# Block 1's norm, transposition and first projection moved into the written-out head, with a new rank table

## The chip, the cores and the metric

One core of one Trainium2 chip runs the kernel. The metric is the device time of one execution in microseconds (us), the median of several runs. The core has a matrix engine (TensorE, in the profile PE for the matmuls and PEld for the loads of their weights), three engines for element-wise work (VectorE is DVE, ScalarE is ACT, GpSimd is POOL), and SyncE (SP), which here only issues data transfers (DMAs). Each engine works through its own list of instructions in order and waits for the others through semaphores. Matmul results go to PSUM, a small memory of eight banks; everything else lies in SBUF.

## What is computed

Input x has 4 sequences of 512 tokens with 256 features. A Mamba layer and a mixture of experts follow one another, each with a layer norm in front and behind and a residual sum:

```python
def _mamba_forward(h, in_proj_w, conv_w, conv_b, x_proj_w, dt_proj_w, dt_proj_b, A, D, out_proj_w):
    x, gate = split(einsum('bld,ed->ble', h, in_proj_w), 2)       # 256 -> 512 + 512
    xt = silu(causal_depthwise_conv4(x) + conv_b)
    ts, Bm, Cm = split(xt @ x_proj_w.T, [16, 32])                 # 16 + 16 + 16
    dt = softplus(ts @ dt_proj_w.T + dt_proj_b)
    state = state * exp(dt * A) + dt * Bm * xt                    # per token, 512 x 16 states
    y = (state @ Cm + xt * D) * silu(gate)
    return y @ out_proj_w.T
def _ffn(xt, ...):
    probs = softmax(xt @ w_router); top 4 of 16 experts, weights normalised -> cw
    g = silu(xt @ we1) * (xt @ we3) * cw;  moe = g @ we2          # hidden 128 per expert
    shared = silu(xt @ ws1) * (xt @ ws3) @ ws2                    # hidden 512
    return shared / 5 + moe * 4 / 5
x = x + layernorm(mamba(layernorm(x)))
x = x + layernorm(ffn(layernorm(x)))
```

All of it is in float32.

## The kernel before

**Blocks.** The 2048 tokens are worked on in 8 blocks of 256 tokens, two per sequence (blocks 0 and 1 are the halves of the first sequence, so block 1 takes over the last three columns of block 0's projection for its convolution, the `tail`, and block 0's last scan states, the `carry`).

For each block n there are these groups of steps:

- The **front**: `stats` (DVE, line 348), `rstd` (four small POOL operations, 354 to 357), `norm` (two ACT passes, 362), `transpose` (PE, 672), `evict` (the ACT copy of the transposed block out of PSUM into `xn_t`, 675), `pad0` (POOL writes the first three columns of the padded tile `xp`, 691 or 693), `in` (PE, 398; two halves m, each four matmuls, which PE carries out as eight instructions), `tail` (the ACT copy into `xp`, 696, and where the sequence goes on the copy of its last columns, 699), `conv` (PE, 413), `sigmoid` (ACT), `silu` (DVE, 430), `x_proj` (PE, 441), `ssm` (ACT, 449), `dt` (PE, 464), `softplus` (ACT, 470), `inputs` (POOL), the gate's `gin`, `gsig`, `gate` (PE 398, ACT 753, DVE 757), and transfers through DRAM that turn the data round (`xg`, `rep`, `bc`).
- The **scans**: 32 slots for each block. A slot takes two exponentials on ACT (`exps`, 500), half of a 128x1024 product on POOL (`dbx`, 512), one scan on DVE (`scan`, 795), one product on DVE (`hc`, 803), and a sum over states on PE (`sum`, 817).
- The **chain**: output projection (PE, 912), norm, residual sum, norm, transposition, the copy `evict2` (ACT, 945), router, and the experts' weights.
- The **experts**: ten steps of two experts each. A step is `h1` and `h3` (PE, 1059), `act` (ACT), `gated` (DVE, 1078), `weighted` and `product` (POOL, 1074 and 1081), and `down` (PE, 1094).

**Who sets the order.** Two parts of the program are ordered in different ways. The **head**, the function `first()`, is written out by hand: it loads the constants, and carries block 0 through its whole front and its first two `exps` and `dbx`. Everything later is a list of **tasks**. Each task has an engine, an estimated duration, the tasks it depends on, the buffers it takes and a **rank**. The planner (`Plan.order`) plays the list through with its own estimates and always takes the task that can start soonest on its engine; within a task's `patience` (in us) a task of lower rank may come first. The result is fixed before the program runs: each engine gets its instructions in the planned order and waits in that order.

A task's rank is the slot at which it is due, plus a shift that the tables `SHIFTS` hold for each kind of task and each block, plus what `NUDGES` holds for one task alone (the table is empty here):

```python
shift, patience = shift_of(name)
rank += shift + NUDGES.get(name, 0.0)
```

So that the planner knows what the head leaves behind, `did(...)` enters tasks as already done.

**Warm-ups.** `warm(n, bank)` (line 320) multiplies the unit matrix n times and throws the result away; each of these matmuls is two PE instructions. The head calls it in places where PE would have nothing to do, and until the first `down` the planner's last loop adds such matmuls wherever its plan leaves PE idle (those go to the bank `po`).

**Buffers.** Tiles with a name share a ring of a fixed number of buffers (`RINGS`): the bank `h` (three PSUM banks for the exponentials and scans), `o` (one), `g` (three, for the experts), `x` (three input blocks), `xn`, `xn_t`, `xp` and others.

**The head's order of loads.** x(0) first, half by SP and half by ACT; ACT then issues both halves of `w_in`; SP issues `chan`, `w_x`, `one_row`, `w_dt`, `a_rep`, `rsel`, `bsel`, then x(1) and x(2), then `w_out` and `w_r`.

Of the kernel before, what the change touches and what calls it, by code (L numbers as in the profile page):

```python
# [9 lines left out]
F32 = mybir.dt.float32  # L10
# [4 lines left out]
P = 128  # L15
# [4 lines left out]
KC = 4  # L20
# [37 lines left out]
    fA=(-0.25, -42.5, 4.25, -39, 39.75, -19.75, 44.5, -1.5),  # L58
    fB=(0, -35.25, -36, 6, 17.25, 55, -7.75, -55),
    fC=(-18.5, -59.25, 7.25, 1.5, -0.5, -12.75, -18, 3.25),  # L60
    fD=(28.25, 18.5, -1, -3.25, 0.25, 38.5, 0.75, -10),
    exps=(3, 34.75, 26.75, -5, -49.5, 44.75, -3.75, 0),
    dbx=(25.75, 11.75, -1.75, -1, 2, 17, 2.75, 12.5),
    scan=(46.75, 18, -13.25, 52, 58.5, 38.75, 48.5, 14.25),
    hc=(8, -37.75, 60, -8, 11, 49.25, -3.75, -17.25),
    keep=(54.75, 0, 25.75, 0, 31.5, 0, 35.75, 0),
    sum=(-18.25, -0.5, 0, 0, 5.25, -6.25, -13.25, 3),
    close=(1.75, 20.5, 2.5, -42.75, -34, 19.5, -5.5, 29),
    ld=(1.25, 34, 20, -0.25, -1.75, -17.5, 33, -9.75),
    bc=(1, 15, 1.5, -14.25, -33.5, 7.5, -5.75, 5),  # L70
    chain=(-4, -7.75, -47.75, -48.25, -17, -9, 8.25, 5.5),
    load=(-8, 9, -14.25, -51.25, -48.5, -60, -23.25, -20.25),
    h1=(60, 18.25, -37.75, -7.75, 9.75, 6.5, 5.75, 6),
    h3=(17.5, 38.75, -48, -19.5, -1.5, -0.75, -1.5, -22.5),
    act=(0, 49.5, 16.5, 3, 4.25, -3, 8.75, 8.25),
    gated=(-11.75, 3, -2, -9.25, 6.75, 2.5, 8.25, 15.5),
    prod=(57, -58.5, 38.75, -3.25, -9.5, -8.25, 0, -11.75),
    down=(-5, 48.5, -31.75, 14.75, -7.25, 6, -1.75, 47.5),
    fin=(16.25, 7, 24.5, 18.25, -2.25, 36.5, -3, 16),
# [3 lines left out]
    fA=(0.1, 0.3, 1.5, 0.1, 1.5, 0.1, 1, 0.1),  # L83
    fB=(0.1, 0.1, 0.1, 0.3, 0.1, 1.5, 1, 0.6),
    fC=(0.1, 0.1, 0.6, 1, 0.3, 0.1, 0.1, 0.1),
    fD=(2.2, 0.1, 0.1, 0.1, 0.1, 1, 0.1, 0.1),
    exps=(0.1, 2.2, 0.3, 0.1, 1.5, 0.3, 0.3, 0.3),
    dbx=(0.3, 0.1, 0.1, 0.1, 0.1, 0.1, 0.1, 2.2),
    scan=(1, 0.6, 0.1, 0.6, 2.2, 0.1, 0.1, 0.1),
    hc=(0.1, 0.1, 2.2, 2.2, 0.3, 0.6, 1.5, 0.1),  # L90
    keep=(1.5, 0.1, 0.1, 0.1, 0.6, 0.1, 1, 0.1),
    sum=(0.3, 1.5, 0.1, 0.1, 0.1, 0.1, 0.1, 0.1),
    close=(0.1, 0.3, 0.3, 0.6, 0.3, 0.3, 0.6, 0.6),
    ld=(1, 1, 1.5, 0.6, 1.5, 0.1, 2.2, 0.6),
    bc=(0.6, 2.2, 0.1, 1.5, 1.5, 0.3, 2.2, 0.6),
    chain=(0.6, 0.6, 0.3, 0.6, 0.1, 0.6, 0.1, 1.5),
    load=(2.2, 1.5, 1, 1.5, 2.2, 2.2, 0.1, 0.1),
    h1=(2.2, 0.3, 0.3, 0.1, 1, 0.1, 0.1, 2.2),
    h3=(0.1, 1, 0.1, 0.1, 0.3, 0.1, 1, 0.3),
    act=(0.1, 2.2, 0.1, 0.3, 0.6, 1, 0.1, 0.1),  # L100
    gated=(0.6, 0.1, 1, 0.6, 0.6, 0.1, 0.3, 0.1),
    prod=(1, 0.1, 1, 0.1, 0.1, 0.1, 0.1, 0.3),
    down=(0.3, 1.5, 0.1, 1, 0.1, 2.2, 0.1, 0.1),
    fin=(0.3, 1, 2.2, 1, 0.6, 2.2, 1.5, 0.1),
# [3 lines left out]

# [143 lines left out]
def mamba_then_moe(ctx: ExitStack, tc: tile.TileContext, a: dict, out: bass.AP):  # L252
# [28 lines left out]
    nc.sync.dma_start(out=chan, in_=a["chan"].rearrange("(c p) k -> p c k", p=P))  # L281
    w_x = const.tile([P, CI, P // 2], F32, name="w_x")
# [17 lines left out]
    for n in range(1, 3):  # L300
        load_x(n)
# [89 lines left out]
    def to_rep(n, m, w, t):  # L391
        nc.sync.dma_start(out=live[n]["rep"][ts(m, 2), :, w].rearrange("j p t -> p j t"), in_=t)

    def in_proj(n, m, bank):
        t = q["in", n, m] = ps.tile([P, 2, U], F32, name=bank)
        for j in range(2):
            for k in range(CD):
                T.matmul(  # L398
# [898 lines left out]
```

## Time and profile before

| what | value |
|---|---|
| median of 3 runs | 695.48 us (695.46 to 695.65) |
| the profiled execution | 695.37 us |
| its span, first to last instruction | 693.6 us |
| mean granted TensorE clock | 0.998 |
| busy: PE, PEld, DVE, ACT, POOL | 674.0, 536.5, 579.3, 495.5, 602.5 us |
| first scan of block 0, first scan of block 1 | 27.0, 96.5 us |
| first expert matmul | 119.6 us |
| last scan | 612.4 us |
| last matmul ends | 688.2 us |

In the views of the profile, a line of the timeline gives the start, the duration, the engine, the line of the kernel, the operation, what it writes and reads, shapes and a count; what stands in brackets is how long the engine was idle before it and who released it. A q behind an engine's name means its sequencer, which issues transfers. Instructions on one engine overlap a little, since they are pipelined; two matmul instructions of 256 columns start 0.216 us apart, though each is shown with 0.38 us.

### The profile page before, as it was taken

What the parts mean: (1) busy time and instruction counts of PE and PEld (TensorE: products, weight loads), DVE (VectorE), ACT (ScalarE), POOL (GpSimd) and SP (SyncE); (2) the same over time, 40 slices, a digit from 0 to 9 for tenths busy, and PEclk for the clock granted to TensorE, in tenths of its full rate; (3) what the DMA queues carried; (4) which work ended last, traced back from release to release, by engine and by line L of the source; (5) the groups of instructions that cost most, each with busy time, mean ns of one, the idle gap of its engine ahead of it and who ended that gap; (6) DMA issues with size and microseconds to landing.
All of it is one profiled execution on the core that took longest, in us unless ns stands there. A gap on an engine that the chain in (4) does not pass through costs nothing.

```text
span 693.6 us, 13321 instructions
## 1 busy us (share of the span) xinstructions
PE 674.0 (97%) x4462; PEld 536.5 (77%) x4462; DVE 579.3 (84%) x821; ACT 495.5 (71%) x1308; POOL 602.5 (87%) x607
## 2 busy tenths in 40 slices
PE   8999898999999999999999999999999999999996
PEld 7867676777878678877777788787777787878885
DVE  3799999999999899999999999889999979952112
ACT  2799979888768778877798867877777757724320
POOL 1597679999999999999999999999999999985553
PEclk9999999999999999999999999999999999999999
DMA  5398675686877596787678867686787764664561
GB/s 175 127 341 283 215 239 172 204 262 186 280 245 226 194 307 236 230 282 265 191 247 276 272 192 228 219 277 231 240 255 251 264 230 140 196 204 131 189 206 46
DMA packets 84840, 155.28 MB, mean 224 GB/s; under 512 B 9858, under 2 KB 33410, under 8 KB 84772
## 3 DMA queue, kind: packets, MB, share of 16 engines
q1 hardware_dynamic: 83940, 153.13, 67.9%
q10 hardware_dynamic: 832, 1.31, 0.5%
q8 instruction: 35, 0.57, 0.3%
q14 instruction: 33, 0.27, 0.1%
HBM read 135.40 MB, written 19.01 MB: 223 GB/s over the span
## 4 chain that ended last, share of the span: by engine, by line
PE 48%; DVE 10%; ACT 7%; POOL 3%; issue 2%; DMA 1%; POOLq 0%; DVEq 0%; ACTq 0%
PE h L1059 25%; PE po L1094 12%; DVE h L795 5%; PE y L817 4%; ACT h L500 3%; DVE hc L803 3%; PE f L912 2%; POOL dbx L512 1%; PE f L1094 1%; PE f L398 1%; DVE q L1078 1%; DMA rep<-rep 1%; PE f L413 1%; ACT h L503 1%; PE f L951 0%
## 5 line engine op out<-in xcount | busy, mean ns | idle before, releaser
L795 DVE TENSOR_TENSOR_SCAN h<-h,dbx 128x512 f32<-128x512 f32 x256 | 308.5, 1221 | 12.0 <-ACT h L503 6.4
L512 POOL TENSOR_TENSOR dbx<-rep,bt 128x1024 f32<-128x1024 f32 x127 | 299.6, 2362 | 13.3 <-DVE h L795 12.8
L1059 PE MATMUL h<-xn_t,w 128*128 128x256 f32 x1280 | 296.0, 382 | 0.2
L500 ACT ACTIVATE h<-rep,a_rep 128x256 f32<-128x256 f32 x512 | 244.5, 478 | 54.7 <-DVE hc L803 42.5
L1059 PEld LDWEIGHTS h<-xn_t,w 128*128 128x128 f32 x1280 | 239.4, 190 | 43.4 <-issue 4.4
L803 DVE TENSOR_TENSOR hc<-h,ct 128x512 f32<-128x512 f32 x256 | 171.6, 683 | 3.8 <-ACT carry L807 1.1
L1094 PE MATMUL po<-w,g 128*128 128x256 f32 x600 | 144.2, 383 | 1.0 <-POOL g L1081 0.8
L1094 PEld LDWEIGHTS po<-w,g 128*128 128x128 f32 x600 | 111.6, 190 | 22.5 <-POOL g L1081 3.9
L1081 POOL TENSOR_TENSOR g<-g,q 128x512 f32<-128x512 f32 x80 | 101.7, 1271 | 5.2 <-DVE q L1078 2.5
L1074 POOL TENSOR_TENSOR g<-g,cwb 128x512 f32<-128x512 f32 x64 | 81.4, 1271 | 19.4 <-ACT g L1071 15.6
L1078 DVE SCALAR_TENSOR_TENSOR q<-th,h 128x512 f32<-128x512 f32 x80 | 54.5, 681 | 49.2 <-PE h L1059 40.4
L1066 ACT ACTIVATE th<-h 128x512 f32<-128x512 f32 x80 | 47.5, 593 | 38.7 <-PE h L1059 38.3
L817 PE MATMUL y<-hc,sel 128*32 128x256 f32 x1024 | 67.5, 385 | 0.0
L817 PEld LDWEIGHTS y<-hc,sel 128*32 128x32 f32 x1024 | 27.5, 109 | 29.0 <-issue 14.6
L503 ACT COPY h<-zero 128x1 f32<-128x1 f32 x256 | 41.7, 163 | 8.2
L398 PE MATMUL f<-xn_t,w_in 128*128 128x256 f32 x176 | 42.6, 385 | 2.2 <-DVE gate L757 1.1
L1071 ACT COPY g<-h 128x512 f32<-128x512 f32 x64 | 37.1, 580 | 9.2 <-PE f L1094 8.7
L398 PEld LDWEIGHTS f<-xn_t,w_in 128*128 128x128 f32 x176 | 32.6, 190 | 10.1 <-ACT xn_t L675 1.7
L807 ACT COPY carry<-h 128x2 f32<-128x2 f32 x128 | 19.8, 160 | 19.2 <-DVE hc L803 13.5
L413 PE MATMUL h<-xp,taps 64*64 64x256 f32 x288 | 29.5, 381 | 0.8 <-DVE xt L430 0.8
L912 PE MATMUL f<-w_out,yg 128*128 128x256 f32 x112 | 26.5, 383 | 1.0 <-DVE xt L430 1.0
L413 PE MATMUL f<-xp,taps 64*64 64x256 f32 x208 | 25.4, 382 | 1.7 <-DVE xt L430 0.9
(178 smaller groups left out, 624.6 us busy)
## 6 DMA issues: line engine op xcount, KB each, us to landing
w<-in_w SPq DMA_DIRECT2D x80, 512.0 KB, 4.9
rep<-rep SPq DMA_DIRECT2D x124, 256.0 KB, 4.5
w<-in_w SPq DMA_DIRECT2D x80, 256.0 KB, 3.8
cwb<-cwd SPq DMA_DIRECT2D x64, 256.0 KB, 4.7
xg<-xg SPq DMA_DIRECT2D x32, 256.0 KB, 4.3
bt<-bc SPq DMA_DIRECT2D x8, 512.0 KB, 5.8
ct<-bc SPq DMA_DIRECT2D x8, 512.0 KB, 5.3
xg<-xt SPq DMA_DIRECT2D x16, 256.0 KB, 4.6
```

Source lines behind the costliest of these rows:

```text
L398: T.matmul(t[:, j, :], w_in[:, k, ts(2 * m + j, P)], q["xn_t", n][:, k, :], start=k == 0, stop=k == CD - 1,)
L413: T.matmul(t[j][half[r ^ j], :], taps[half[r], 2 * m + j, k, :], q["pad", n, m][half[r], j, k : k + U], start=k == 0, stop=k == KC - 1,)
L500: S.activation(h[:, j, :], dt[:, m, 0, :], AF.Exp, scale=a_rep[:, c, g, m : m + 1])
L512: G.tensor_tensor(t[:, m], reps[n * CI + c][:, m, 1, :], bt[:, m], ALU.mult)
L795: V.tensor_tensor_scan(flat, flat, dbx[:, ts(p, NJ), :].rearrange("p j t -> p (j t)"), 0.0, ALU.mult, ALU.add)
L803: V.tensor_tensor(hc, expo[k], ct, ALU.mult)
L817: T.matmul(ys[n, c][m * CS : (m + 1) * CS, :], sel, hcs[k][:, j, :], start=g == 0, stop=g == SG - 1,)
L1059: T.matmul(t[:, j, :], weights[i][:, j, ts(CD * w + k, P)], x[:, k, :], start=k == 0, stop=k == CD - 1,)
L1074: G.tensor_tensor(gs[i], gs[i], cws[i], ALU.mult)
L1078: V.scalar_tensor_tensor(t, hid[i, "th"], 1.0, hid[i, 1], ALU.add, ALU.mult)
L1081: G.tensor_tensor(gs[i], gs[i], hid[i, "q"], ALU.mult)
L1094: T.matmul(acc[n][t] if n == N - 1 else acc[n][:, t, :], gs[i][:, j, ts(t, P)], weights2[i][:, j, :], start=m == 0 and j == 0 and (t == 0 ...
```

## The change

The head takes over the first steps of block 1, and the planner's tables are replaced.

1. x(1) is loaded behind `chan`, ahead of `w_x`, instead of behind `bsel`.
2. In the head, block 1's statistics and `rstd` are put behind block 0's normalization; its two normalizing ACT passes (into a tile of the ring `o`) behind `make_taps()`; its transposition (into a bank `h`) behind block 0's convolutions; its copy into `xn_t` on DVE (into a tile of the ring `g`) behind `silu(0, 0)`. ACT did this copy before.
3. The first half of block 1's input projection, `in(1, 0)`, is cut into its four matmuls. One goes behind the second, one behind the fourth column of block 0's `x_proj`, each followed by two warm-ups, where four and two warm-ups were; the other two go behind `dt_proj`. The copy into `xp` is made by DVE, and the two warm-ups on `y` are gone. POOL copies both halves' tails into `xp`.
4. The planner no longer has `stats`, `rstd`, `norm`, `transpose`, `evict`, `pad0` of block 1 nor `in` and `tail` of its first half; `did` tells it so.
5. All values of `SHIFTS` and `PATIENCE` are new, and `NUDGES` gets some 90 entries.

```diff
 SHIFTS = dict(
-    dbx=(25.75, 11.75, -1.75, -1, 2, 17, 2.75, 12.5),
-    scan=(46.75, 18, -13.25, 52, 58.5, 38.75, 48.5, 14.25),
-    chain=(-4, -7.75, -47.75, -48.25, -17, -9, 8.25, 5.5),
-    h1=(60, 18.25, -37.75, -7.75, 9.75, 6.5, 5.75, 6),
+    dbx=(-4, -5, 51, 30.25, 46.5, 55, 30.75, 48.5),
+    scan=(45.25, 60, 0, 48.75, 46.75, 60, 23.5, 33.75),
+    chain=(-36, -22.75, -16, -28.25, 17.5, -47.75, -1, -4.5),
+    h1=(-4, 60, 53, 40.5, 57.25, -19, -6, 4.75),
...
 NUDGES = {
+    ("rep", 0, 1, 0): 6.5, ("xg", 0, 0, 1): 19.5, ("conv", 1, 1): -23.5, ("inputs", 1, 1): -24,
+    ("pad0", 2, 0): 2, ("gsig", 2, 1): -24.5, ("stats", 3): 13.25, ("in", 3, 1): 11.75,
...
 }
...
     nc.sync.dma_start(out=chan, in_=a["chan"].rearrange("(c p) k -> p c k", p=P))
+    load_x(1)
...
-    for n in range(1, 3):
-        load_x(n)
+    load_x(2)
...
-    def in_proj(n, m, bank):
-        t = q["in", n, m] = ps.tile([P, 2, U], F32, name=bank)
+    def in_parts(n, m, t):
+
+        q["in", n, m] = t
         for j in range(2):
             for k in range(CD):
                 T.matmul(
                     t[:, j, :], w_in[:, k, ts(2 * m + j, P)], q["xn_t", n][:, k, :],
                     start=k == 0, stop=k == CD - 1,
                 )
+                yield
+
+    def in_proj(n, m, bank):
+        for _ in in_parts(n, m, ps.tile([P, 2, U], F32, name=bank)):
+            pass
...
+        mr = rstd_of(stats_of(xs[1]))
         xn_t = q["xn_t", 0] = ring(work, [P, CD, U], "xn_t")
...
         make_taps()
+        xn1 = ring(work, [P, NU, D], "o")
+        normalize(xn1, tiles_of(xs[1]), mr)
...
             conv(0, m, (("po", "f"), ("h1", "h3"))[m])
+        t = ps_e.tile([P, CD, U], F32, name="h")
+        for k in range(CD):
+            for i in range(NU):
+                T.transpose(t[:, k, ts(i, P)], xn1[:, i, ts(k, P)], ident)
         sigmoid(0, 0)
         silu(0, 0)
+
+        q["xn_t", 1] = ring(work, [P, CD, U], "g")
+        V.tensor_copy(q["xn_t", 1], t)
...
         silu(0, 1)
+        parts = in_parts(1, 0, ps_e.tile([P, 2, U], F32, name="h"))
+        for m in range(2):
+            xp = q["pad", 1, m] = ring(work, [P, 2, KC - 1 + U], "xp")
+            G.tensor_copy(xp[:, :, 0 : KC - 1], tails.pop((1, m)))
+
+        def some(c):
+            next(parts)
+            warm(2, "f")
+
         S.activation(spare, zero, AF.Softplus)
-        x_proj(0, "y", lambda c: warm(5 - c, "f"))
+        x_proj(0, "y", some)
...
         dt_proj(0, ("po", "h1"))
+        for _ in parts:
+            pass
+        V.tensor_copy(q["pad", 1, 0][:, :, KC - 1 :], q["in", 1, 0])
         b0 = ps.tile([P, U], F32, name="f")
...
         V.tensor_copy(first_b, b0)
-        warm(2, "y")
         softplus(0)
...
-        if n:
+        if n > 1:
             if n > 2:
                 once(key("x"), "SP", 0.5, lambda: load_x(n), (), [("x", key("x"))], (), 256)
...
-            for m in range(2):
+            for m in range(n == 1, 2):
```

## The prediction

> **What bounds the kernel now.** I read the chain that ended last first, then busy time by stage, then the timeline of the head and of the first scans. The chain is mostly TensorE:
>
> ```profile
> PE 48%; DVE 10%; ACT 7%; POOL 3%; issue 2%; DMA 1%; POOLq 0%; DVEq 0%; ACTq 0%
> ```
>
> One table over four stretches: the head up to the first scan, block 0's scans up to the first expert matmul (119.60), up to the last scan, and the rest. Columns: length, then busy us (and instructions) of PE, PEld, DVE, ACT, POOL, then clock, DMA share, GB/s.
>
> ```profile
> 0.00:27.00 27.00, 24.86 (x199) 20.77 (x200) 11.39 (x36) 11.86 (x24) 4.20 (x15) 1.00 0.51 157
> 27.00:119.60 92.60, 83.57 (x754) 63.82 (x752) 88.22 (x118) 81.89 (x227) 75.34 (x83) 1.00 0.74 243
> 119.60:612.40 492.80, 489.59 (x3133) 386.68 (x3134) 461.09 (x632) 381.55 (x1020) 478.25 (x457) 1.00 0.72 235
> 612.40:694.00 81.60, 75.99 (x381) 65.25 (x379) 18.59 (x40) 20.25 (x39) 44.66 (x54) 0.98 0.49 158
> ```
>
> From 119.60 PE stands 492.80 - 489.59 = 3.2 us in 493, with POOL 14.6 behind it. So the end is: the time at which expert work starts, plus all PE work left then, plus few stalls, plus 5.4 (last matmul 688.2 to 693.6). Before 119.60 PE is not full: idle 92.60 - 83.57 = 9.0, and 146 of its instructions there are warm-ups (L320), 18 of which take 2.17 us, so 146 x 0.112 = 16.4. That is 25.4 us of spare PE, because DVE (88.22 of 92.60) paces block 0's scans.
>
> A second bound is close. Block 7's last scan starts at 612.4, its router input is copied at 632.2, and ten steps of h1, h3 and down at 3 x 1.73 us follow: 632.8 + 51.9 = 684.7, against PE's real end of 688.2. Whatever saves PE more than 3.5 us must also bring the last scan forward.
>
> **The head, part by part.** The added work: statistics of x(1) (DVE 0.70, row L348), four small POOL operations (0.19, 0.22, 0.71, 0.20; 1.5 with gaps, seen for block 2 at 32.16), two normalizing ACT passes (1.09), eight transposing PE instructions (0.47), a 512-wide DVE copy out of PSUM (0.69, row L540), eight input-projection PE instructions (8 x 0.216 = 1.73), the copy to xp (DVE 0.69), two tail copies (POOL 0.32). Removed there: 4 warm-ups, 8 PE instructions (0.9 us).
>
> The load of x(1) is now the third on SP's queue instead of after bsel. The nearest row is w_x, issued at 1.64 and landed 5.9 us later at 7.5, when the 1 MB of w_in on ACT's queue was through. x(1) is 256 KB, 128 KB more; at the some 350 GB/s of 3 to 7 us that is +0.4: 7.9. DVE asks for it at 8.03, between xn and xn_t. Late x(1) would hold the xn_t copy (8.69), behind which taps and the projection queue; bounds 7.1 (half of 350 GB/s from 5.66, where w_in's first half had landed) and 9.5 (after w_in, at the 127 GB/s of the page's second slice); I take no delay. w_x and the constants slide by 0.7 at most: w_x then lands at 8.3, used at 16.61; rsel (10.93), used at 22.02. [...]
>
> Statistics then end at 8.73, POOL at 10.3, the ACT passes at 11.4, which pushes the ACT copy to xp from 10.93 to 11.4; it ends at 12.0, before the convolution's 12.55. That much is covered. The transposition lies in PE's 0.38 wait before 16.61, and its rest ahead of the second x_proj column (17.0). Not covered is this:
>
> ```profile
> 16.48 0.47 DVE L430 SCALAR_TENSOR_TENSOR xt<-f,chan,sig 128x256 f32<-128x256 f32 x1
> 16.87 0.28 DVE L551 TENSOR_SCALAR sig<-sig 128x256 f32<-128x256 f32 x1
> 17.25 0.88 DVE L430 SCALAR_TENSOR_TENSOR xt<-h,chan,sig 128x256 f32<-128x256 f32 x2
> 17.37 1.16 PE L320 MATMUL f<-ident 128*128 128x128 f32 x8
> 18.46 0.66 PE L441 MATMUL y<-xt,w_x 128*64 128x128 f32 x8
> 19.05 0.71 PE L320 MATMUL f<-ident 128*128 128x128 f32 x4
> 19.17 0.37 ACT L449 ACTIVATE ssm<-y,one_row 128x128 f32<-128x128 f32 x1
> 26.39 0.70 DVE L348 BATCH_NORM_STATS2 st<-x 128x6 f32<-128x512 f32 x1
> 27.01 2.32 DVE L795 TENSOR_TENSOR_SCAN h<-h,dbx 128x512 f32<-128x512 f32 x2
> ```
>
> The new copy stands on DVE between silu(0,0) and sig: 16.95 to 17.65. sig goes to 17.65, silu(0,1) ends at 18.85 instead of 18.13. On PE the first projection matmul waits for that copy to 17.9 and lasts 0.43, two warm-ups 0.45, so x_proj's second half starts at 19.0, not 18.46 (+0.55), and ssm with it. The second matmul with its warm-ups (0.88) stands ahead of dt_proj: 19.0 + 0.6 + 0.88 + 0.1 = 20.6 against 19.69 (+0.9). Two more (0.86) and b0 (0.44) precede the spread matmuls, whose softplus comes 0.9 later too: 23.1 against 22.05, **+1.05** for everything up to the first scan. Bounds: 0 (if the order hides all) and 1.7 (all 1.73 exposed). Against it: x(1)'s statistics held DVE from 26.39 until the first scan, although that scan's dbx was there at 26.10 and the last rep copy ended at 26.47; they are gone: **-0.5**. Head: +0.5.
>
> **The stream.** Block 1 no longer takes there ACT 1.09 + 0.59 + 0.56 = 2.2, POOL 1.5 + 0.3, PE 0.47 + 1.73 = 2.2. PE's and ACT's share is worth nothing by itself: DVE paces this stretch. POOL's is:
>
> ```profile
> 32.16 0.19 POOL L354 TENSOR_SCALAR rstd<-st 128x2 f32<-128x2 f32 x1
> 33.56 0.32 POOL L691 COPY xp<-tail 128x6 f32<-128x6 f32 x2
> 33.88 2.38 POOL L512 TENSOR_TENSOR dbx<-rep,bt 128x1024 f32<-128x1024 f32 x1
> 36.28 2.35 DVE L795 TENSOR_TENSOR_SCAN h<-h,dbx 128x512 f32<-128x512 f32 x2 [0.53 <-POOL dbx L512]
> 40.13 1.23 DVE L795 TENSOR_TENSOR_SCAN h<-h,dbx 128x512 f32<-128x512 f32 x1 [0.32 <-POOL dbx L512]
> ```
>
> The dbx stands behind block 1's rstd and pads, and scans wait 0.53 and 0.32 for it: **-0.85** (bounds 0 and 3.1, all of DVE's idle time from 27 to 97).
>
> **The new table.** It reorders every planned instruction, and no row prices it; only the room can be read. (a) PE's 2.2 us now done in the head pay if block 4's front is pulled into the place: bounds 0 and -2.2, taken **-1.1**. (b) Between out_proj of block 0 (99.73) and the first expert matmul lie 19.9 us, of which the steps themselves (out 1.56, two statistics 0.70, two rstd 1.3, two norms 1.05, add 1.28, turn 0.9, copy 0.58) are 10.4 and hand-overs some 2. Some 7 could go. The chain's shift for block 0 falls from -4 to -36, so it passes more of its rivals; POOL's 2.36 dbx still cannot be interrupted. Bounds -7 and +2.4 (one more dbx ahead): taken **-1.0**. (c) After 119.60: 3.2 idle on PE, bounds -3.2 and +7 (below), taken 0, since it is full already.
>
> Sum: 0.5 - 0.85 - 1.1 - 1.0 = **-2.45**. Span 693.6 to 691.2. The profiled run took 695.37 (1.8 around its span), the median is 695.48, so **693.0**. The forecast's own range is 688 to 694.1. A measurement can tell about 0.2%, 1.4 us, from no change: 694.1 to 696.9 counts as the same.
>
> **Rivals.** *Nothing moves* (chance 0.17): PE swaps warm-ups for moved matmuls, DVE paces block 0 as before, the experts start near 119.6 and PE's later work is untouched. For it: 25.4 us of spare PE; against it: the 0.85 and the 7. Time +0.5 - 0.85 = 695.1.
>
> *POOL falls behind* (0.20, slower). Between 119.60 and 612.40 POOL is busy 478.25 of 492.80, and serves both scans (dbx, 2.36) and experts (weighted, product, 1.27 each) in fixed order. If the new order puts one expert product ahead of a dbx once per block that DVE then awaits, as in the trace's three waits of DVE for L514 (2.9 us, 1.0 each), seven blocks lose up to 7 x 1.0; with half of it made good later, +3.5: **699**. It decides from the point where the last scan starts later than 612.4 + 3.5. Against it: PE has other work during such waits.
>
> *Late x(1)* (0.07): landing at 9.5 holds xn_t, taps and the convolution by 1.5; head +2.0, nothing returned but 0.3: **697.2**.
>
> **Numbers.** Forecast 0.56. Low end: 688.5, with (a) in full and half of (b), plus 0.5 of (c): 695.48 - 0.35 - 2.2 - 3.5 - 0.5 = 688.9, rounded down. High end 698.5, below the worst half of the POOL rival. Left out: about 0.07 below, 0.11 above. Faster 0.56, same 0.17, slower 0.27.
>
> **What would show it.** First scan at 27.5 (27.0 to 28.2); second half of x_proj at 19.0; statistics of x(1) at 8.0 without a DMA wait; no DVE wait for dbx near 36; first L1059 matmul at 117 to 119; fewer than 146 warm-ups on po; last scan between 609 and 613; PE idle after the first expert matmul still about 3 us. Wrong, if the experts start after 120, or if the PE idle time after their start exceeds 6 us.

## The result, and the profile after

The changed kernel takes 696.62 us (median of 20 runs, 695.82 to 698.56). The kernel before, run beside it, takes 695.80 us (20 runs, 695.03 to 696.41). The ratio is 1.0014 with a 95% interval of 1.0008 to 1.0020. So it became 0.8 us slower, less than the 0.2% that were to count as a difference, where the forecast was 2.5 us faster.

Before traces are compared, one thing has to be taken out. The first input projection matmul of block 0, the first work that needs x, `w_in` and the norm, starts at another time in each execution, and everything behind it slides along: from 8.90 to 9.56 us in five executions with the old order of loads, from 8.54 to 9.84 in twelve with the new one. In most of them it isn't the loads that set it, but the head's first 40 warm-ups, which stand on PE ahead of this work and take between 6.1 and 7.5 us (`e4_load_alone` below). So all times below that are called *relative* are counted from that matmul. It began at 8.90 before and 8.69 after.

| relative time, us | before | after | difference |
|---|---|---|---|
| first scan | 18.11 | 19.78 | +1.67 |
| scan of slot 31, the last of block 0 | 85.33 | 87.48 | +2.15 |
| first expert matmul | 110.70 | 112.12 | +1.42 |
| last scan | 603.46 | 603.96 | +0.50 |
| end of the span | 684.74 | 685.43 | +0.69 |

The head lost 1.67 us where the prediction had 0.5, and the rest won 1.0 where it had 2.95. The chain of waits can't be set beside the one of before. In the execution profiled after, it breaks off a few steps from the end:

```profile
DVE 0%; issue 0%; DVEq 0%
```

So the stages have to do. These are the same four stretches of the kernel after, cut at its own first scan, first expert matmul and last scan (length, then busy us and instructions of PE, PEld, DVE, ACT, POOL, then clock, DMA share and GB/s):

```profile
0.00:28.47 28.47, 25.95 (x203) 21.64 (x204) 13.21 (x39) 12.85 (x26) 5.92 (x21) 1.00 0.48 150
28.47:120.80 92.33, 84.37 (x787) 62.98 (x785) 90.41 (x116) 84.64 (x230) 75.71 (x79) 1.00 0.76 255
120.80:612.60 491.80, 488.56 (x3099) 386.70 (x3096) 457.14 (x632) 375.89 (x1016) 477.35 (x460) 1.00 0.70 234
612.60:694.00 81.40, 76.09 (x382) 65.67 (x380) 18.08 (x39) 19.09 (x38) 42.96 (x50) 0.98 0.48 153
```

Read the second row against the one of before. It is a quarter of a microsecond shorter, no more, although DVE's idle time in it fell from 92.60 - 88.22 = 4.4 us to 1.9. What DVE waited for there, first before, then after (what was waited for, us in total, how often, longest):

```profile
DVE h L795 <- ACT h L503: 2.5, 2, 1.3
DVE h L795 <- POOL dbx L512: 0.9, 2, 0.5
DVE gate L757 <- ACT sig L753: 0.6, 1, 0.6
DVE xt L430 <- ACT sig L425: 0.2, 1, 0.2
```

```profile
DVE h L855 <- ACT carry L867: 0.4, 2, 0.2
DVE h L855 <- ACT h L534: 0.3, 1, 0.3
DVE hc L863 <- ACT carry L867: 0.2, 1, 0.2
```

The waits for `dbx` are gone, as predicted, and nearly all of those for ACT. DVE's timeline where the scans had waited 0.53 and 0.32 us has no bracket any more:

```profile
35.10 1.22 DVE L855 TENSOR_TENSOR_SCAN h<-h,dbx 128x512 f32<-128x512 f32 x1
36.36 0.69 DVE L863 TENSOR_TENSOR hc<-h,ct 128x512 f32<-128x512 f32 x1
36.97 1.22 DVE L855 TENSOR_TENSOR_SCAN h<-h,dbx 128x512 f32<-128x512 f32 x1
...
39.62 1.22 DVE L855 TENSOR_TENSOR_SCAN h<-h,dbx 128x512 f32<-128x512 f32 x1
```

But DVE is busy 2.2 us longer before the first expert matmul, although the durations of what it does there add up to only 0.3 us more (97.2 us before, 97.5 after): 43 scans instead of 42, and some small steps more or fewer. What changed is by how much its instructions overlap: 97.2 - 88.2 = 8.9 us before, 97.5 - 90.4 = 7.1 after. In the lines above, the product of 36.36 stands directly behind the scan of 35.10 and starts 0.04 us after that scan's end. Before, two scans stood in a row, and the product behind them started 0.08 us before the second one had ended:

```profile
27.01 2.32 DVE L795 TENSOR_TENSOR_SCAN h<-h,dbx 128x512 f32<-128x512 f32 x2
29.25 0.67 DVE L803 TENSOR_TENSOR hc<-h,ct 128x512 f32<-128x512 f32 x1
```

Counted in order, 23 of block 0's 32 products now stand directly behind the scan that they read, where 1 did before. So the new order closed the waits and lost overlap in their place: from the first scan to slot 31 it takes 67.70 us instead of 67.22. That the products' place is the reason is read from these starts; no run tests it alone.

From slot 31 to the router the new order needs 2.35 us less (a relative 108.56 - 87.48 = 21.08 instead of 108.76 - 85.33 = 23.43), but then lets a convolution pass ahead of the first expert matmul:

```profile
117.25 1.06 PE L1011 MATMUL h<-w_r,xn_t 128*128 128x16 f32 x8 [0.51 <-ACT xn_t L1005]
118.92 0.43 PE L444 MATMUL f<-xp,taps 64*64 64x256 f32 x2 [0.60 <-ACT tail L758]
...
120.80 1.99 PE L1119 MATMUL h<-xn_t,w 128*128 128x256 f32 x8
```

So of the 2.35 us 0.73 are left at the first expert matmul. In the third row PE is idle for as little as before, 491.80 - 488.56 = 3.2 us, but it has 1.03 us less to do: ahead of the experts it now carries out 224 instructions of convolutions instead of 192, and 48 of `dt` instead of 32.

The other half of the story is the head. The timeline of the kernel after, where the order of PE and DVE is to be read:

```profile
7.50 0.69 DVE L373 BATCH_NORM_STATS2 st<-x 128x6 f32<-128x512 f32 x1
...
18.47 0.66 PE L472 MATMUL y<-xt,w_x 128*64 128x128 f32 x8
...
21.81 0.59 ACT L501 ACTIVATE dt<-h 128x512 f32<-128x512 f32 x1
...
22.39 0.69 DVE L614 COPY xp<-h 128x512 f32<-128x512 f32 x1 [3.94 <-PE h L424]
...
23.00 0.41 DVE L619 COPY th<-f 128x256 f32<-128x256 f32 x1
23.51 1.10 PE L631 MATMUL f<-dt,w 128*128 128x256 f32 x4 [0.72 <-issue]
...
27.85 0.71 DVE L373 BATCH_NORM_STATS2 st<-x 128x6 f32<-128x512 f32 x1
28.47 1.21 DVE L855 TENSOR_TENSOR_SCAN h<-h,dbx 128x512 f32<-128x512 f32 x1
```

Three things stand in it. x(1)'s statistics start at 7.50 without a wait, and the second half of `x_proj` starts at 18.47, where it started at 18.46 before: both good. Softplus ends at 22.40, yet PE starts the spread matmul (L631, which turns `dt` round for the first scan) only at 23.51, after 0.72 us of idling. "issue" says that the profile names no releaser, so one has to look for who touches the same bank: the spread writes bank `f`, `b0` lies in bank `f`, and its copy to `th` (L619) ends at 23.41. That copy stood on DVE behind the new copy into `xp`. And ahead of the first scan, where x(1)'s statistics stood, there is again a line of statistics (27.85): those of block 2.

### The profile page after: what moved, and what is told of

Its sections match the earlier page's. It is cut to its first block, busy times and chain, and to the rows that moved or that the text cites. A ratio compares the mean times of both kernels' runs of the same rounds, so it can differ in the third digit from the quotient of the medians.

```text
span 694.1 us, 13331 instructions
## 1 busy us (share of the span) xinstructions
PE 675.0 (97%) x4464; PEld 537.0 (77%) x4464; DVE 578.8 (83%) x823; ACT 492.5 (71%) x1306; POOL 601.9 (87%) x607
## 5 line engine op out<-in xcount | busy, mean ns | idle before, releaser
L531 ACT ACTIVATE h<-rep,a_rep 128x256 f32<-128x256 f32 x512 | 244.8, 478 | 66.4 <-DVE hc L863 53.1
L424 PE MATMUL f<-xn_t,w_in 128*128 128x256 f32 x160 | 38.7, 385 | 1.8 <-DVE gate L817 0.8
L424 PEld LDWEIGHTS f<-xn_t,w_in 128*128 128x128 f32 x160 | 29.6, 190 | 8.5 <-ACT carry L867 1.2
```

The lines of the kernel that those rows point to most:

```text
L424: T.matmul(t[:, j, :], w_in[:, k, ts(2 * m + j, P)], q["xn_t", n][:, k, :], start=k == 0, stop=k == CD - 1,)
L531: S.activation(h[:, j, :], dt[:, m, 0, :], AF.Exp, scale=a_rep[:, c, g, m : m + 1])
```

## The experiments

The same claims were in dispute throughout. One account: the head's delay comes from the order of PE and DVE around bank `f`, and the scans of block 0 pass it on undiminished to the experts, from where PE alone sets the end. Its rivals: the 25 us of spare PE ahead of the experts swallow such a delay and the loss lies in the new order; or the fixed order passes on any delay, wherever it arises; or the loads or the clock explain it. The quoted texts number such theories; which of them was at stake stands in front of each quotation, and what became of it behind it. The ratios in the tables are the comparison's own estimate from the rounds; the quotient of two medians differs from them by up to 0.08%. The kernel before had medians of 696.02, 695.67, 695.84 and 695.64 us in the four sets.

### First set: the head, the table, the loads

Is it the copy in front of `first_b`? `b0` and its copy go ahead of the two last projection matmuls and the copy into `xp`; the rest is the kernel after.

```diff
-        for _ in parts:
-            pass
-        V.tensor_copy(q["pad", 1, 0][:, :, KC - 1 :], q["in", 1, 0])
         b0 = ps.tile([P, U], F32, name="f")
...
         V.tensor_copy(first_b, b0)
+        for _ in parts:
+            pass
+        V.tensor_copy(q["pad", 1, 0][:, :, KC - 1 :], q["in", 1, 0])
         softplus(0)
```

> The changed kernel with one move in its head: b0's matmuls and the copy to first_b stand ahead of the last two projection matmuls and of the DVE copy to xp. Bank f, which the first spread matmul writes, is then free when softplus ends. Theory 1 (the head's loss is that wait and goes through to the end): first spread matmul 23.5 to about 22.6, first scan 28.5 to about 27.5, first expert matmul 120.8 to about 119.8, time 1.0 us under the changed kernel, so about 0.2 us under the kernel before (ratio to before 0.9997). Theory 2 (the head is covered by the 26 us of spare PE time before the experts, and the new table is what costs): first scan as early as in theory 1, but the time within 0.3 us of the changed kernel (ratio 1.0014).

Can head and table be priced apart by crossing them? `e2_new_head_old_table` is the kernel after with the old `SHIFTS`, `PATIENCE` and an empty `NUDGES`; `e3_old_head_new_table` the kernel before with the new ones.

> The new head and the shorter list of tasks, with the old values of SHIFTS and PATIENCE and no NUDGES. Theory 1: the head's 1.5 us come through here as well, and the old values were not made for this list, so 1 to 3 us above before (ratio 1.0015 to 1.004). Theory 2: the head costs nothing, so within 0.5 us of before, and below the changed kernel.

> The old head and the old list of tasks, with the new values of SHIFTS, PATIENCE and NUDGES. Theory 1: the first scan is back at 27.0 to 27.6 and the new values pull as before, so at or below before (ratio 0.998 to 1.001). Theory 2: the new values are what costs, so above before by 0.5 us or more (ratio over 1.0007).

Does the place of x(1)'s load move the start of the head? The kernel before with this alone:

```diff
     nc.sync.dma_start(out=chan, in_=a["chan"].rearrange("(c p) k -> p c k", p=P))
+    load_x(1)
...
-    for n in range(1, 3):
-        load_x(n)
+    load_x(2)
```

> The kernel before with the one edit that x(1) is loaded third on SP's queue. In the changed kernel chan landed at 4.81 instead of 5.26 and the head ran 0.45 us ahead at the statistics, 0.2 ahead at the convolutions. If the load order alone does that, statistics of x(0) start at about 5.05 and the first scan at about 26.8; theory 1: the time falls by about 0.2 us (ratio 0.9997); theory 2: no change that shows.

| kernel | first scan, relative | first expert matmul, relative | end, relative | median, us | ratio to before |
|---|---|---|---|---|---|
| `e1_b0_first` | 18.83 | 112.67 | 685.70 | 696.85 | 1.0004 (0.9995 to 1.0013) |
| `e2_new_head_old_table` | – | – | – | 738.45 | 1.0609 (1.0594 to 1.0623) |
| `e3_old_head_new_table` | – | – | – | 735.45 | 1.0566 (1.0551 to 1.0580) |
| `e4_load_alone` | 18.12 | 110.70 | 684.79 | 695.58 | 0.9998 (0.9989 to 1.0006) |

**The bank.** The timeline of `e1_b0_first`, at the same place:

```profile
22.51 0.59 ACT L501 ACTIVATE dt<-h 128x512 f32<-128x512 f32 x1
22.67 0.42 DVE L616 COPY th<-f 128x256 f32<-128x256 f32 x1 [3.52 <-PE f L614]
...
23.33 1.03 PE L631 MATMUL f<-dt,w 128*128 128x256 f32 x4
...
23.54 0.69 DVE L619 COPY xp<-h 128x512 f32<-128x512 f32 x1 [0.44 <-PE h L424]
```

Now the spread follows softplus (23.10) by 0.23 us, and the first scan comes 0.95 us earlier. So 0.95 of the 1.67 us was that one copy. At the end of the span nothing of it is seen: from the first scan on to the experts 1.5 us were lost again. The granted clock, in two stretches of this execution, shows where:

```profile
115.00:120.00 5.00, 3.89 (x43) 2.58 (x47) 5.00 (x9) 4.81 (x16) 4.84 (x7) 0.90 0.50 171
120.00:125.00 5.00, 5.00 (x34) 3.37 (x29) 3.64 (x14) 3.83 (x11) 4.64 (x8) 0.76 0.36 107
```

At half the clock, 0.10 x 5 us and 0.24 x 5 us missing are 1.0 + 2.4 = 3.4 us of half clock, from 119.0 to 122.4. PE's timeline just ahead of it:

```profile
117.00 1.06 PE L1011 MATMUL h<-w_r,xn_t 128*128 128x16 f32 x8 [0.51 <-ACT xn_t L1005]
118.67 0.45 PE L444 MATMUL f<-xp,taps 64*64 64x256 f32 x2 [0.60 <-ACT tail L758]
...
118.94 0.61 PE L444 MATMUL f<-xp,taps 64*64 64x256 f32 x2
...
119.33 0.65 PE L444 MATMUL f<-xp,taps 64*64 64x256 f32 x2
```

From 106 us on no gap is longer than 0.60 us. What stands there is block 0's router, eight matmuls of 16 columns, between two short waits; then the convolution's pairs follow each other by 0.39 to 0.43 us instead of the 0.21 to 0.22 that the kernel after has there: half the clock. 8 of the 11 runs of this kernel have a mean clock of 0.995 or 0.996, like this one, and three have 0.998; the median is of the former. In `e12_no_router_warm` below the same two stretches are at 0.84 and 0.82, which is 0.8 + 0.9 = 1.7 us missing, or 3.4 us of half clock again.

Neither the waits nor the router decide it alone. The profiled execution of the kernel after has the same eight matmuls between the same two waits, 0.51 and 0.60 us, and its clock stayed at 1.00 from 110 to 124 us. In the kernel before PE idles for 0.76 us up to 115.10; in the 3.41 us from 114.52 on it is busy for 2.15 us, with 0.27 us of router in them, and the clock stayed at 1.00 there, too. In the 3.4 us ahead of the fall in `e1_b0_first` it is busy for 2.3. So why the clock fell in one execution and not in the others is not shown; what the second set tests is whether more matmuls around the router keep it up.

**The table.** The two crossings cost 42 and 39 us. That answers nothing about the 0.8 us: these tables are only good with the list of tasks that they were made for. The last set takes another way.

**The load.** x(1) in its new place changes no time: the first projection matmul came 0.94 us later than in the execution before, and scans, experts and end 0.94 to 1.00 later with it; relative to it nothing differs by more than 0.06, and the ratio's interval holds 1. The 0.94 us don't come from the loads, since x(0) was normalized earlier than in the execution before. What came later was PE, first in the kernel before, then in `e4_load_alone`:

```profile
1.34 6.60 PE L320 MATMUL f<-ident 128*128 128x128 f32 x40 [1.34 <-POOL ident masks.py:199]
7.30 0.73 DVE L523 TENSOR_SCALAR xn<-x,st,rstd 128x256 f32<-128x256 f32 x2 [1.11 <-POOL rstd L520]
8.00 0.44 PE L531 MATMUL f<-ident,xn 128*128 128x128 f32 x2
```

```profile
1.34 7.54 PE L320 MATMUL f<-ident 128*128 128x128 f32 x40 [1.34 <-POOL ident masks.py:199]
7.06 0.73 DVE L523 TENSOR_SCALAR xn<-x,st,rstd 128x256 f32<-128x256 f32 x2 [1.11 <-POOL rstd L520]
8.94 0.44 PE L531 MATMUL f<-ident,xn 128*128 128x128 f32 x2
```

The same 40 warm-ups take 6.60 us and 7.54. They start 0.213 us apart up to 5.3 us in the one and up to 7.3 us in the other, and 0.111 apart from there on. In 13 of the 17 profiled executions the transposition (L531) starts within 0.06 us of the last warm-up's end; in the other four it waits for the norm.

### Second set: what passes a delay on

Does spare PE swallow a delay of the head? The kernel before, with ten more warm-ups (2.2 us of PE) ahead of softplus's spread:

```diff
         V.tensor_copy(first_b, b0)
-        warm(2, "y")
+        warm(12, "y")
         softplus(0)
```

> The kernel before with ten more warm-ups on y ahead of the spread matmuls, 20 PE instructions of 0.112 us: the first scan 2.2 us later (about 29.3), nothing else. Theory 1 (what the head loses goes through to the end, since DVE paces block 0's scans): every scan, the first expert matmul and the end 2.2 us later, ratio 1.0025 to 1.0035. Theory 2 (spare PE time before the experts covers it): first expert matmul less than 0.7 us later, ratio under 1.0010.

Is it the router that costs the clock? `e1_b0_first` with five warm-ups around block 0's router:

```diff
         def router():
+            if n == 0:
+                warm(2, "po")
             t = z["r"] = ps.tile([P, NU, E], F32, name=bank)
...
+            if n == 0:
+                warm(3, "po")
```

> The head with b0 first, as before, and five warm-ups around block 0's router matmuls (two ahead, three behind), where PE stood 0.58 and 0.60 us idle and where the run with b0 first had the clock at half for 3.4 us, from 118.6 to 122. Theory 1: no run has that half clock any more (mean clock 0.998 or more in all), and the time is at the level of those runs of b0 first that had none (694.7 to 695.5), about 0.7 us under before, ratio 0.9985 to 0.9995. Theory 2: clock and time spread as they did (0.996 in most runs), ratio 1.0000 to 1.0013.

Do block 2's statistics ahead of the first scan cost their 0.7 us? `e6_b0_first_router_warm` with this task emitted behind the second scan:

```diff
-    for t in plan.order():
+    ordered = plan.order()
+    late = ordered.pop(next(i for i, t in enumerate(ordered) if t["name"] == ("stats", 2)))
+    ordered.insert(1 + next(i for i, t in enumerate(ordered) if t["name"] == ("scan", 1)), late)
+    for t in ordered:
```

> The same, and block 2's statistics (DVE, 0.71 us) moved from ahead of the first scan to behind the second one. Its reader on POOL comes at 41.6 only. Theory 1: the first scan 0.5 us earlier than with the statistics in front, and the end 0 to 0.5 us earlier, since DVE still has to do the work within the same stretch; ratio 0.998 to 0.9993. Theory 2: the first scan earlier, the end unchanged.

Does the pair of warm-ups behind the second projection matmul hold up `dt_proj`? `e7_stats_later` without it:

```diff
             next(parts)
-            warm(2, "f")
+            if c == 1:
+                warm(2, "f")
```

> The same again, and the two warm-ups behind the fourth x_proj column taken out, which stand ahead of dt_proj: dt_proj starts at 19.7 instead of 20.1 after the same start of the loads. Theory 1: first scan another 0.4 us earlier (about 26.6 to 26.8), end 0.4 us earlier, ratio 0.9975 to 0.9988. Theory 2: end unchanged. If fewer warm-ups let the clock fall in the head, the granted clock of 20 to 30 us shows it.

| kernel | first scan, relative | slot 31, relative | first expert matmul, relative | end, relative | median, us | ratio to before |
|---|---|---|---|---|---|---|
| `e5_delay` | 20.00 | 87.20 | 112.58 | 686.64 | 697.56 | 1.0026 (1.0015 to 1.0037) |
| `e6_b0_first_router_warm` | 18.82 | 86.53 | 111.26 | 684.53 | 695.41 | 0.9998 (0.9990 to 1.0007) |
| `e7_stats_later` | 18.21 | 86.63 | 111.36 | 684.64 | 695.68 | 1.0001 (0.9992 to 1.0010) |
| `e8_no_second_warm` | 17.77 | 86.18 | 110.90 | 684.21 | 695.29 | 0.9992 (0.9983 to 1.0001) |

`e5_delay` settles the main question. Against before, the first scan is 1.89 us late, slot 31 1.87, the first expert matmul 1.88 and the end 1.90. Not a tenth of it is swallowed, though PE has 146 instructions of warm-ups, 16 us, in between. A delay of the head is worth its full length.

`e6_b0_first_router_warm` shows that the clock was the loss: its first scan is that of `e1_b0_first`, its end 1.17 us earlier, and the same two stretches are at full clock:

```profile
115.00:120.00 5.00, 5.00 (x63) 3.62 (x58) 5.00 (x9) 4.84 (x15) 4.92 (x4) 1.00 0.51 152
120.00:125.00 5.00, 4.66 (x26) 3.94 (x26) 4.81 (x16) 4.84 (x14) 4.77 (x10) 1.00 0.38 134
```

All 11 runs have a mean clock of 0.998 or more. Against the kernel after, the first scan is 0.96 us earlier and the end 0.90. So the bank `f` is worth 0.9 us at the end.

`e7_stats_later` is a miss for the account that took the scans' start for the pace of all: the first scan comes 0.61 us earlier, slot 31 0.10 later. `e8_no_second_warm` returns the pair whole: 0.44 us in the head, 0.43 at the end.

### Third set: where DVE's time counts

Is DVE the pace in block 0, and has it slack once the experts run? Three products `hc` are done twice, which is 3 x 0.683 = 2.05 us of DVE: in block 0 of the kernel before (`e9_double_hc_block0`, slots 8, 16 and 24), and in block 4 of the kernel after (`e10_double_hc_block4`, slots 136, 144 and 152). They write the same values twice.

```diff
         V.tensor_tensor(hc, expo[k], ct, ALU.mult)
+        if k in (8, 16, 24):
+            V.tensor_tensor(hc, expo[k], ct, ALU.mult)
```

> The kernel before, with the DVE product hc of slots 8, 16 and 24 (block 0) done twice: 3 x 0.68 = 2.0 us more DVE work before the experts start, results the same. Theory 1 (DVE paces block 0's scans, and what it loses there goes through): DVE has 4.4 us idle in that stretch in 92.6, so most comes through: first expert matmul and end 1.2 to 2.0 us later, ratio 1.0017 to 1.003. Theory 2 (25 us of spare PE time cover it): end less than 0.5 us later, ratio under 1.0007.

> The changed kernel, with hc of slots 136, 144 and 152 (block 4) done twice: the same 2.0 us of DVE work, but after the experts' start, where the changed kernel's scans run 6 to 12 us ahead of the kernel before. Theory 1 (from there on PE alone sets the end, so the scans' lead is worth nothing): scans of blocks 5 and 6 up to 2 us later, end within 0.5 us of the changed kernel, ratio to before 1.0008 to 1.0022. Theory 2 (DVE paces throughout): end 2 us later, ratio 1.0035 to 1.0050.

Is there a hole in the head for block 2's statistics? `e8_no_second_warm` with its statistics in the head, the planner's task standing where it was in the kernel after and doing nothing:

```diff
         silu(0, 1)
+        q["early"] = stats_of(xs[2])
         parts = in_parts(1, 0, ps_e.tile([P, 2, U], F32, name="h"))
...
-                mine["mv"] = stats_of(xs[n])
+                mine["mv"] = q["early"] if n == 2 else stats_of(xs[n])
```

> b0 first, router warm-ups, no second pair of warm-ups, and block 2's statistics now in the head, behind silu(0,1), where DVE idles for 3 us (x(2) lands at 12.5); the task stays in the plan and does nothing. Theory 1: unlike their move behind the second scan, this takes 0.7 us of DVE work out of the stretch that DVE paces, so the whole stream comes 0.5 to 0.7 us earlier than in the run without the second warm-ups: end about 694.7 as a median, ratio to before 0.998 to 0.9992. Theory 2: end as in that run (0.9992).

Are the router's warm-ups still needed when the head is shorter? `e12_no_router_warm` is `e8_no_second_warm` without them.

> The run without the second pair of warm-ups, but also without the five warm-ups around the router matmuls. If those keep the clock up: some of the runs at a mean clock of 0.996 and 1.2 to 1.9 us longer again (ratio 0.9995 to 1.001). [...]

| kernel | first scan, relative | slot 31, relative | first expert matmul, relative | end, relative | median, us | ratio to before |
|---|---|---|---|---|---|---|
| `e9_double_hc_block0` | 18.11 | 86.21 | 111.57 | 686.11 | 697.30 | 1.0019 (1.0010 to 1.0028) |
| `e10_double_hc_block4` | 19.78 | 87.49 | 112.13 | 686.90 | 698.10 | 1.0028 (1.0018 to 1.0039) |
| `e11_stats2_in_head` | 17.77 | 85.79 | 110.52 | 683.79 | 695.04 | 0.9981 (0.9972 to 0.9991) |
| `e12_no_router_warm` | 17.76 | 86.18 | 112.27 | 685.32 | 696.18 | 0.9996 (0.9988 to 1.0005) |

Of 2.05 us more DVE work in block 0, only 0.88 reach slot 31 and 0.87 the first expert matmul; DVE had 4.4 us of idling to lose part of it in. Yet 1.37 reach the end, so 0.50 more arise behind the experts' start. In block 4 of the kernel after, 1.47 of the 2.05 us reach the end. There the scans run 8 us ahead of the kernel before (slot 127 at a relative 299.25 instead of 307.50), and PE is idle 0.7% of the time; by "PE alone sets the end" the work should have been free. That account falls. In an order that is fixed in advance, each engine meets the others at the same places, and being ahead of another kernel is no slack.

`e11_stats2_in_head` beats both kernels: by the medians 0.8 us below the kernel before, with an interval that leaves out 1, and by the relative ends 0.95 below before and 685.43 - 683.79 = 1.64 below after. DVE's timeline in it shows the hole, and the first scan without statistics in front:

```profile
19.28 0.70 DVE L373 BATCH_NORM_STATS2 st<-x 128x6 f32<-128x512 f32 x1
22.43 0.42 DVE L618 COPY th<-f 128x256 f32<-128x256 f32 x1 [2.46 <-PE f L616]
...
26.75 0.69 DVE L636 COPY rep<-po 128x512 f32<-128x512 f32 x1 [0.17 <-PE po L633]
27.36 1.22 DVE L857 TENSOR_TENSOR_SCAN h<-h,dbx 128x512 f32<-128x512 f32 x1
```

Its first scan starts where that of `e8_no_second_warm` does; the 0.42 us come from the statistics no longer standing between later scans. `e12_no_router_warm` ends 1.11 us later than `e8_no_second_warm`, and 6 of its 11 runs have a mean clock of 0.996 or 0.997: the warm-ups are needed.

### Fourth set: the moved work and the new order, apart

What would the statistics' removal be worth in the old order? The kernel before with those of blocks 1 and 2 done in the head, behind block 0's convolutions, and nothing else changed:

```diff
             conv(0, m, (("po", "f"), ("h1", "h3"))[m])
+        for n in range(1, 3):
+            q["early", n] = stats_of(xs[n])
         sigmoid(0, 0)
...
-                mine["mv"] = stats_of(xs[n])
+                mine["mv"] = q["early", n] if n < 3 else stats_of(xs[n])
```

> The kernel before, with the statistics of x(1) and x(2) (DVE, 2 x 0.70) done in its head behind the convolutions, where DVE idles from 13.4 to 16.1 (both blocks have landed by 12.7); the tasks stay in the plan and do nothing. Theory 1 (DVE work taken out of block 0's stretch comes back at half its size or more, as the doubled hc did the other way): first scan 0.5 us earlier, end 0.7 to 1.2 us earlier, ratio 0.9983 to 0.9990. Theory 2 (other engines set that stretch's length): end within 0.3 us, ratio over 0.9995.

What is the moved work worth without a new order, and the order without the moved work? `e14_new_head_old_order` has the head of the kernel after, but the planner plans with the old tables and the old list of tasks; those which the head has done stay in the plan and do nothing when their turn comes. `e15_mended_head_old_order` is the same with the head of `e11_stats2_in_head`, the router's warm-ups included.

```diff
+            if n == 1:
+                stats = rstd = norm = transpose = evict = lambda: None
...
+                if n == 1:
+                    return
...
+                if (n, m) == (1, 0):
+                    return
```

> The changed kernel's head, with the old order of everything behind it; block 1's moved steps stay in the plan and do nothing. Theory 1 (moved work alone pays little, the new order alone little more): first scan 1.2 to 1.7 us later after the same start of the loads, of which the moved work gives back 0.5 to 1.0: end 0.5 to 1.2 us after the kernel before, ratio 1.0007 to 1.0017, as the changed kernel. Theory 2 (the new order earned the whole 1.0 us): nothing given back, end 1.7 us later, ratio 1.002 to 1.003. Theory 3 (the new order lost): end at or below before.

> The mended head (b0 first, one pair of warm-ups less, block 2's statistics in it, warm-ups around the router) with the old order behind it. Theory 1: first scan 0.4 us earlier than before, and 0.7 to 1.2 us given back by the moved work: ratio 0.9980 to 0.9990, like the mended head with the new order (0.9981), so that the new order adds nothing that shows. Theory 2 (the new order is worth 1 us): ratio 0.9992 to 1.0000. Theory 3 (the new order costs): under 0.9975.

| kernel | first scan, relative | slot 31, relative | first expert matmul, relative | end, relative | median, us | ratio to before |
|---|---|---|---|---|---|---|
| `e13_old_stats_in_head` | 17.50 | 85.29 | 110.66 | 684.72 | 695.86 | 0.9999 (0.9990 to 1.0008) |
| `e14_new_head_old_order` | 19.16 | 87.37 | 112.73 | 687.10 | 697.34 | 1.0020 (1.0011 to 1.0029) |
| `e15_mended_head_old_order` | 17.76 | 84.16 | 110.24 | 684.26 | 695.55 | 0.9997 (0.9988 to 1.0006) |

`e13_old_stats_in_head` brings the first scan 0.61 us forward and the end 0.02. DVE's timeline says who took it:

```profile
28.02 1.23 DVE L797 TENSOR_TENSOR_SCAN h<-h,dbx 128x512 f32<-128x512 f32 x1 [0.24 <-POOL dbx L512]
...
36.43 2.35 DVE L797 TENSOR_TENSOR_SCAN h<-h,dbx 128x512 f32<-128x512 f32 x2 [1.28 <-POOL dbx L512]
```

The second scan now waits for POOL's `dbx`, and the wait near 36, 0.53 us before, has become 1.28. POOL stands right behind DVE; what one gives the other takes.

`e15_mended_head_old_order` takes the same work out of the stream as `e11_stats2_in_head`, in the old order. Its first scan is 0.35 us earlier than before, and slot 31 1.17 us: so the moved work, together with block 2's statistics, returns 0.82 us in block 0's scans. The statistics without the moved work returned nothing there (`e13_old_stats_in_head`: slot 31 0.04 us earlier). At the router `e15_mended_head_old_order` is still 1.17 us ahead (a relative 107.59 against 108.76), but its first expert matmul comes only 0.46 us earlier, and its end 0.48. Its own warm-ups take the rest: the old order has three behind the router already, and three more were put there. First before, then `e15_mended_head_old_order`:

```profile
119.11 0.43 ACT L970 ACTIVATE lg<-h,red 128x16 f32<-128x16 f32 x2
119.60 4.58 PE L1059 MATMUL h<-xn_t,w 128*128 128x256 f32 x20
```

```profile
117.71 1.91 PE L320 MATMUL po<-ident 128*128 128x128 f32 x12
118.25 0.43 ACT L1011 ACTIVATE lg<-h,red 128x16 f32<-128x16 f32 x2
119.45 0.81 PE L1100 MATMUL h<-xn_t,w 128*128 128x256 f32 x3
```

Before, the first expert matmul starts 0.06 us after ACT has read the router's bank (119.54). In `e15_mended_head_old_order` ACT is done at 118.68, and PE still has warm-ups to do. Without the added ones the experts could start 0.7 us earlier; that is an estimate from these lines. From their start to the end it is 574.0 us, so the end could come at a relative 683.6, about where `e11_stats2_in_head` has it (683.79). So the 0.47 us by which `e11_stats2_in_head` ends earlier don't show that the new order is better.

With the head of the kernel after, the two orders differ by 1.67 us in the relative end, but the profiled execution of `e14_new_head_old_order` has a clock of 0.83 from 40 to 50 us, which is 3.4 us at half, and 2 of its 11 runs have its mean clock of 0.996. By the medians, each against the kernel before beside it, the difference is (697.34 - 695.64) - (696.62 - 695.80) = 0.88 us; by the ratios, 1.0020 and 1.0014, it is 0.4, and their intervals overlap. What the new order is worth as a whole is not shown. Where it wins and loses can be read: from the first expert matmul to the end six kernels with the old order take 574.0 to 574.4 us and seven with the new one 573.0 to 573.3 (those with doubled products left out). From the first scan to slot 31 the new order takes 68.02 us with the mended head (`e11_stats2_in_head`), the old one 66.40.

## Why the prediction was wrong

It was wrong in sign: 0.8 us slower, where 2.45 faster was forecast; the forecast's likeliest case failed, and the time lies in the band that was to count as the same, 1.5 us above *Nothing moves*. Two steps failed most: the head (+0.5, measured +1.67) and POOL's relief (-0.85, measured +0.48 in block 0's scans). Step by step:

- **The order in the head (+1.05)** had the right sign and too small a size: 1.67, and the step that failed is "23.1 against 22.05". It followed PE's list and counted the copy into `xp` as DVE work with nothing behind it. But the copy of `b0` is behind it on DVE, and the spread writes `b0`'s bank: 0.95 us (`e1_b0_first`). The pair of warm-ups ahead of `dt_proj` was 0.44 (`e8_no_second_warm`); with it `dt_proj` starts 0.65 later in relative time, not 0.9. The remaining 0.28 go with the second half of `x_proj`, which is 0.22 later in relative time, not 0.55.
- **x(1)'s statistics (-0.5)** did not come. The new order puts those of block 2 in the same place. And where they are gone in the old order the end doesn't move (`e13_old_stats_in_head`, 0.02): the step took a gain at the first scan for one at the end.
- **x(1)'s load (0)** was right: no wait, no price. It landed at 6.82, 5.2 us after its issue: before the 7.9 worked out from the row of `w_x`, and before the 7.1 that was that estimate's lower bound.
- **POOL's relief (-0.85)**: the waits near 36 and 40 went, as predicted, but from the first scan to slot 31 it took 0.48 us longer, since DVE's instructions overlap less in the new order (shown above). Removed waits were counted as time, under a table whose order of DVE had not been looked at. In the old order the moved work and block 2's statistics did return 0.82 there (`e15_mended_head_old_order`).
- **(a) PE's 2.2 us refilled (-1.1)**: came nearly as taken. PE has 1.03 us less to do from the first expert matmul to the last scan (488.56 instead of 489.59), since more convolutions and `dt` come ahead of it. The sign that had been named for it was wrong: warm-ups on `po` ahead of the experts rose from 146 to 152 instructions instead of falling.
- **(b) The chain (-1.0)**: from slot 31 to the first expert matmul 25.37 us became 24.64, so -0.73. Together with the longer scans that leaves 0.25 from the first scan to the experts, where 1.85 had been forecast. They start at 120.8, and "the experts start after 120" had been named as a sign of failure.
- **(c) After the experts' start (0)**: from the first expert matmul to the end 574.04 us became 573.31, so -0.73; that is (a)'s gain, less 0.19 behind the last scan. PE's idling up to the last scan, 3.2 us, is as predicted, and the last scan, at 612.6 (609 to 613 predicted), too.
- **"From 119.60 PE alone"**, on which (a), (b) and (c) stood, fell with `e10_double_hc_block4`: PE is full, but DVE's work there is on the path as well.

The sum as measured: head +1.67, block 0's scans up to slot 31 +0.48, from there to the first expert matmul -0.73, from there to the end -0.73; together +0.69.

*Nothing moves* was nearest, by luck: PE's work behind the experts' start did change, and both of its terms, the head's +0.5 and POOL's -0.85, were wrong. *POOL falls behind* did not happen in its form, since the last scan came before its bound of 615.9. But its sign was there: between the first expert matmul and the last scan DVE waited 13.6 us for `dbx`, where it had waited 2.9, while its idling there rose only from 31.7 to 34.7 us. That POOL is next in line shows in `e13_old_stats_in_head`, too. *Late x(1)* did not happen.

## What to carry to other kernels

When work is put into an "idle place" of one engine, walk through every bank and buffer that it stands in front of on the other engines' queues: here a 0.69 us copy on an idle DVE held a bank that PE needed, and cost 0.9 us. In this program, whose order is fixed in advance, a delay at the start was passed on whole (`e5_delay`: 1.89 us at the first scan, 1.90 at the end), however much slack an engine shows later. A wait that is removed returns time only if the next engine in line, here POOL, is not right behind (`e13_old_stats_in_head`: the first scan came 0.61 us earlier, the end 0.02), and if the new order of the waiting engine's own instructions costs nothing (0.48 us here, up to slot 31). Price a re-ordering from crossings that keep the list of tasks, and look whether what is added to a crossing (here warm-ups) stands on the path itself; a table tried on another list says nothing.

## What the runs showed of the hardware that was not expected

In `e1_b0_first` the matmul clock fell to half for one stretch of 3.4 us although PE had no gap above 0.60 us in the 13 us ahead of it; just ahead of it stand eight matmuls of 16 columns between waits of 0.51 and 0.60 us. 8 of its 11 runs and 6 of the 11 of `e12_no_router_warm` have so low a mean clock, 0.995 to 0.997. With five 128-column warm-ups around those matmuls all 44 runs of four kernels of that order have 0.998 or more. The loss cost 1.1 to 1.2 us of 695, more than the change itself. Of the 20 runs of the kernel after, three have such a mean clock, and two of them are its slowest, 698.49 and 698.56 us.

The same program starts its first real work up to 1.3 us earlier or later from one execution to the next (8.54 to 9.84 us), and the whole trace slides with it. In 13 of 17 executions this is by when the head's warm-ups go over from one start every 0.213 us to one every 0.111 us, at 4.4 us in the earliest of them and at 7.3 in the latest; a difference of that size between two traces means nothing until it is taken out.
